# Where the adjacency's byte blocks are made in two fused graph-attention layers

## The chip, the cores and the metric

The kernel runs on one core of one Trainium2 chip. The time is the device time of one execution in microseconds (us); of several runs the median is given. A profile is one separate execution with the hardware profiler on. Engine names in the profile: PE is TensorE (PEld its weight loads), DVE is VectorE, ACT is ScalarE, POOL is GpSimd, SP is SyncE, which here only issues DMAs. A line such as L586 is a line of the kernel.

## The reference

A graph of 3327 nodes with 512 features passes two attention layers, then one binarized linear layer. Cut to what matters:

```python
for l in range(2):                                   # attention layers
    proj = x @ W[l]; Wh, Ws = split(proj, 2)         # 512 -> 2 x 512
    scores = Wh @ Ws.T                               # 3327 x 3327
    a = softmax(scores, axis=-1) * adj
    x = leaky_relu(a @ Wh + x, 0.01)
h = layernorm(x0 + x)
xw = max(sign(h), 0) @ sign(weight).T
out = layernorm(h + relu(adj @ xw))                  # adj once more
```

`adj` holds zeros and ones as 32-bit floats. All matmuls of the attentions are in 32-bit floats; the last product with `adj` is made from one-byte copies of `adj` and 16-bit values.

## The kernel before, in words

Scores are kept transposed: nodes j of the keys on the partitions, queries i along the free axis. The 26 tiles of 128 nodes form `NQ = 13` pairs. Every 256 x 256 block product, of scores and of values, is made with seven half-size products in place of eight (Strassen's scheme in Winograd's form), with sums of operands made beforehand. That is why each block has "sums" next to it.

A **full step** `(g, q)` is one 256 x 256 block: query pair g, key pair q; there are 169 of them in an attention, numbered i = 13 g + q. `values` (L820) makes its seven products into accumulators that live through a row g. Before that, in the steps ahead of it, the block goes through `shift` (L739: column maximum subtracted, DVE), `exponential` (L744, L745, ACT), `running` (L750: sum for the softmax, DVE), `masked` (L755: times `adj`, DVE) and `sums` (L793 to L796, POOL).

Scores run ahead of values by `LOOK = 30` half steps, because a row needs its maximum over all q before the first exponential. `ahead` lists these half steps: column block c (two rows g), key pair q, and s = 0 or 1. Half step s = 0 makes four of the seven products, s = 1 the other three (L586), into three banks `pZ`, `pX`, `pY`; ACT copies a bank out (L603, L638) before TensorE adds the next product to it, and DVE makes the final sums (L613, L628, L634) and the running maximum `top` (L654, L656). After the last q of a column block the maximum over the partitions is found by `column_max` (L687 to L707).

The loop over v runs from -34 to 168. In v the scores of half step u = v + 30 are made, and the values of step v if v is not negative. So **steps with scores alone** are v = -30 to -1; in them only scores and maxima are made, until the first rows' `shift` at v = -3. Within one v all work is sorted by a hand-written fraction (0.0 for `shift` of step v + 3, 0.12 for its exponential, 0.4 for `masked` of step v + 2, 0.6 to 0.62 for its byte block, and so on), and each engine gets its instructions in that order. The queues of SP and POOL are in order of issue too: in each v SP issues the load of `ws` (L801), then of `adj` for step v + 4 (L723; L115 and L117 where rows are cut), then `xs` and `gs` for the scores ahead (L577, L568).

The **byte blocks** are what the last layer needs of `adj`. Where an `adj` tile is on the chip anyway for `masked`, DVE makes four sums of its quarters as bytes (`halved_sums`, L775) and tests that all elements are zero or one (`exact`, L784), ACT casts three quarters (`halved`, L761, L762), and in the next v POOL writes the 112 KB block to memory (`keep_blocks`, L778). The byte tile `ab` has two buffers, the `adj` tile four. Each of the 169 blocks is made once: attention 0 makes those with q even (91), attention 1 those with q odd (78). Before, a block is made in its own step if g < 9; the blocks of rows 9 to 12 (28 and 24 of them) are spread over earlier steps of the other parity, which load a second `adj` tile for it.

The last rows of attention 1 and the last layer (L1134) follow; they are not touched.

## Time and profile before

| what | value |
|---|---|
| runs before (3) | median 2616.8 us, 2616.53 to 2617.85 |
| profiled execution | 2613.73 us, its span 2611.9 us |
| granted TensorE clock | 0.999 |
| first score product to first value product, attention 0 | 184.7 to 276.6 us |
| the same, attention 1 | 1400.5 to 1492.6 us |
| last value product of attention 1 | 2471 us |
| DMA moved | 639.15 MB, 245 GB/s on average |

The span runs from the first to the last instruction; the execution's time has 1.8 us around it. A busy TensorE is counted from the modelled ends of pipelined matmuls, so for lost time the count of matmuls in a window is the better measure. In the timeline a line gives start, duration, engine, line, operation, tiles and, in brackets, the idle time of the engine just before it and what ended it. Groups of byte-block work in the page:

```profile
L784 DVE SCALAR_TENSOR_TENSOR adj<-adj 128x512 f32<-128x512 f32 x169 | 139.8, 827 | 25.4 <-ACT ab L762 8.9 <-ACT u L603 0.5 <-DVE ab L775 0.5
L775 DVE TENSOR_TENSOR ab<-adj 128x128 fp8e4<-128x128 f32 x338 | 118.0, 349 | 29.2 <-DMA adj_d<-ab 28.6 <-POOL as L793 0.4
L775 DVE TENSOR_TENSOR ab<-adj,ab 128x128 fp8e4<-128x128 f32 x169 | 86.5, 512 | 0.0
L775 DVE TENSOR_TENSOR ab<-ab,adj 128x128 fp8e4<-128x128 fp8e4 x169 | 79.3, 469 | 5.8
```

The columns are line, engine, operation, tiles, shapes and count, then busy us and mean ns, then idle us before them by cause.

### The profile page before, as it was taken

The page shows a single profiled execution, that of the slowest core. Times are in us where ns is not written, and L with a number is a line of the kernel's source. Part 1 is how long each engine was busy: PE and PEld are TensorE (multiplying, and loading weights), DVE is VectorE, ACT ScalarE, POOL GpSimd, SP SyncE. Part 2 cuts the span into 40 slices and gives each one's busy share as a digit, 9 for nine tenths or more (in the row PEclk, how much of TensorE's full clock was granted, in tenths as well). Part 3 has the DMA queues.
Part 4 walks back from the last instruction along what each step waited for, and adds up shares of the span by engine and source line. Part 5 has one row for each costly group of instructions (what it writes and reads, how often), then busy time and mean ns, then how long its engine had stood idle before and what let it go on. Part 6 is the DMA issues. An engine that isn't in the chain of part 4 may idle for free. (4 is left out here: it accounts for less than half of the span.)

```text
span 2611.9 us, 40070 instructions
## 1 busy us (share of the span) xinstructions
PE 2578.8 (99%) x12511; PEld 2234.7 (86%) x12536; DVE 2109.5 (81%) x4422; ACT 799.8 (31%) x1978; POOL 1091.7 (42%) x2025
## 2 busy tenths in 40 slices
PE   9999999999999999999999999999999999999998
PEld 7888888888888888887888888888888888888787
DVE  6754888899888996768874689989899898777976
ACT  3323332333323332221332333333333333222143
POOL 3640343444434444456662044444444444454610
PEclk9999999999999999999999999999999999999999
DMA  6855777777777877698865678777787777678775
GB/s 216 293 193 180 241 241 265 241 268 251 261 240 236 276 239 237 223 265 252 300 242 179 224 225 283 249 250 258 239 281 247 246 263 237 231 260 262 262 252 182
DMA packets 309783, 639.15 MB, mean 245 GB/s; under 512 B 35048, under 2 KB 177986, under 8 KB 308027
## 3 DMA queue, kind: packets, MB, share of 16 engines
q1 hardware_dynamic: 273868, 530.29, 62.8%
q0 software_dynamic: 35664, 106.18, 11.0%
q8 instruction: 103, 1.69, 0.3%
q14 instruction: 118, 0.96, 0.1%
q10 hardware_dynamic: 30, 0.03, 0.0%
HBM read 529.69 MB, written 106.67 MB: 244 GB/s over the span
## 5 line engine op out<-in xcount | busy, mean ns | idle before, releaser
L586 PE MATMUL pZ<-gs,xs 128*128 128x256 f32 x2496 | 636.9, 379 | 3.0 <-ACT u L603 2.8
L793 POOL TENSOR_TENSOR as<-s 128x128 f32<-128x128 f32 x338 | 162.7, 481 | 1052.6 <-DVE s L755 873.2
L586 PEld LDWEIGHTS pZ<-gs,xs 128*128 128x128 f32 x2496 | 473.0, 190 | 71.3 <-ACT u L603 6.3
L820 PE MATMUL acc<-ws,s 128*128 128x256 f32 x1352 | 402.4, 379 | 0.1
L820 PE MATMUL acc<-wh,s 128*128 128x256 f32 x1352 | 355.7, 379 | 0.7 <-DVE s L755 0.4
L820 PE MATMUL acc<-ws,as 128*128 128x256 f32 x1352 | 348.0, 380 | 4.2 <-POOL as L795 4.1
L745 ACT ACTIVATE s<-s 128x512 f32<-128x512 f32 x338 | 213.2, 631 | 394.3 <-DVE s L739 393.3
L586 PE MATMUL pY<-gs,xs 128*128 128x256 f32 x1248 | 320.8, 379 | 6.0 <-ACT p L603 6.0
L820 PEld LDWEIGHTS acc<-ws,as 128*128 128x128 f32 x1352 | 256.1, 190 | 45.7 <-POOL as L795 8.6
L820 PEld LDWEIGHTS acc<-wh,s 128*128 128x128 f32 x1352 | 256.6, 190 | 36.7 <-DVE s L755 1.9
L820 PEld LDWEIGHTS acc<-ws,s 128*128 128x128 f32 x1352 | 255.7, 190 | 35.5 <-DVE h L855 1.3
L586 PEld LDWEIGHTS pY<-gs,xs 128*128 128x128 f32 x1248 | 236.6, 190 | 40.0 <-ACT p L603 7.9
L656 DVE TENSOR_TENSOR top<-top,s 128x512 f32<-128x512 f32 x286 | 199.9, 713 | 72.9 <-ACT s L643 52.6
L739 DVE TENSOR_TENSOR s<-s,off 128x512 f32<-128x512 f32 x338 | 246.8, 730 | 0.6
L755 DVE TENSOR_TENSOR s<-s,adj 128x512 f32<-128x512 f32 x338 | 239.5, 709 | 8.6 <-DMA adj<-in_adjT_dram 0.6
L750 DVE TENSOR_TENSOR total<-total,s 128x512 f32<-128x512 f32 x312 | 230.3, 738 | 0.0
L795 POOL TENSOR_TENSOR as<-s 128x128 f32<-128x128 f32 x338 | 202.1, 598 | 26.5
L603 ACT COPY u<-pZ 128x256 f32<-128x256 f32 x312 | 115.5, 370 | 308.0 <-PE pZ L586 304.9
L820 PE MATMUL acc<-wh,as 128*128 128x256 f32 x676 | 202.5, 381 | 0.0
L794 POOL TENSOR_TENSOR s<-s 128x128 f32<-128x128 f32 x338 | 182.9, 541 | 27.4
L796 POOL TENSOR_TENSOR as<-s,as 128x128 f32<-128x128 f32 x338 | 183.0, 541 | 26.5
L628 DVE TENSOR_TENSOR s<-p,u 128x256 f32<-128x256 f32 x156 | 66.5, 427 | 137.6 <-ACT u L603 136.9
(214 smaller groups left out, 3886.8 us busy)
## 6 DMA issues: line engine op xcount, KB each, us to landing
ws<-ws_d SPq DMA_DIRECT2D x338, 512.0 KB, 3.8
xs<-xs_d SPq DMA_DIRECT2D x182, 512.0 KB, 5.7
adj<-in_adjT_dram SPq DMA_DIRECT2D x324, 256.0 KB, 4.3
xs<-xs_d SPq DMA_DIRECT2D x156, 384.0 KB, 6.2
gs_d<-gsp POOLq DMA_DIRECT2D x88, 256.0 KB, 3.1
gs<-gs_d SPq DMA_DIRECT2D x12, 1792.0 KB, 10.9
adj_d<-ab POOLq DMA_DIRECT2D x169, 112.0 KB, 3.9
ahl<-adj_d SPq DMA_DIRECT2D x78, 224.0 KB, 5.0
```

The lines of the kernel that those rows point to most:

```text
L586: nc.tensor.matmul(ch[bank], xs[c, q, a][:, k], gs[c][:, b, k], start=(start and k == 0), stop=(k == 1), skip_group_check=True,)
L603: nc.scalar.copy(ch[name], ch[bank])
L656: nc.vector.tensor_tensor(top[i], top[i], t, ALU.max)
L739: nc.vector.tensor_tensor(s, s, off[g].to_broadcast([P, 2, HW]), ALU.subtract)
L745: nc.scalar.activation(sc[g, q], sc[g, q], AF.Exp)
L750: nc.vector.tensor_tensor(total[g], total[g], sc[g, q], ALU.add)
L755: nc.vector.tensor_tensor(s, s, adj[g, q], ALU.mult)
L793: nc.gpsimd.tensor_tensor(s3, a11, a21, ALU.subtract)
L794: nc.gpsimd.tensor_tensor(a21, a21, a22, ALU.add)
L795: nc.gpsimd.tensor_tensor(s2, a21, a11, ALU.subtract)
L796: nc.gpsimd.tensor_tensor(s4, a12, s2, ALU.subtract)
L820: nc.tensor.matmul(acc[g][i // 2][:, i % 2], a[i], b[i], start=(q == 0 and i % 2 == 0), stop=(q == NQ - 1), skip_group_check=True,)
```

## The change

The steps in which the blocks are made are chosen anew. Of each attention, 14 blocks are moved to the steps with scores alone: they get the keys -27, -25, ..., -1, so their `adj` is loaded at v = key - 4, they are made at v = key - 2 (-29 to -3), and written at v = key - 1. In attention 0 these are the blocks of rows 11 and 12. In attention 1 they are first the six blocks with q = 11 and g odd (in the steps with these keys a column maximum is found), and then the last eight of the others (row 12, and q = 9 and 7 of row 11). All other blocks are made in their own step, those of rows 9, 10 and, in attention 1, the first three of row 11 too. No full step makes a block of another step any more, so second loads of `adj` in full steps go: 28 and 24 extra loads become 14 and 14.

```diff
-        first = NQ * (NQ - 4)
         mine = [i for i, e in enumerate(steps) if e[1] % L == l]
-        room = [i for i, e in enumerate(steps[:first]) if e[1] % L != l][2:]
-        late = [i for i in mine if i >= first]
-        blocks = {i: steps[i] for i in mine if i < first}
-        blocks.update(
-            {room[n * len(room) // len(late)]: steps[i] for n, i in enumerate(late)}
-        )
+        alone = list(range(4 - LOOK, 1, 2))
+        moved = [i for i in mine if l and steps[i][1] == NQ - 2 and steps[i][0] % 2]
+        moved += [i for i in mine[::-1] if i not in moved][: len(alone) - len(moved)]
+        blocks = {i: steps[i] for i in mine if i not in moved}
+        blocks.update({i - 1: steps[j] for i, j in zip(alone, moved)})
...
             if 0 <= v + 4 < len(steps):
                 load_adj(*steps[v + 4])
-                if blocks.get(v + 4, steps[v + 4]) != steps[v + 4]:
-                    load_adj(*blocks[v + 4])
+            elif v + 4 in blocks:
+                load_adj(*blocks[v + 4])
...
-                of = blocks.get(v + 2)
-                if of:
-                    work += [
-                        (0.6, lambda: halved_sums(*of)), (0.62, lambda: exact(*of)),
-                        (0.61, lambda: halved(*of)),
-                    ]
-                    after.append((0.5, lambda of=of: keep_blocks(*of)))
+            if v + 2 in blocks:
+                of = blocks[v + 2]
+                work += [
+                    (0.6, lambda: halved_sums(*of)), (0.62, lambda: exact(*of)),
+                    (0.61, lambda: halved(*of)),
+                ]
+                after.append((0.5, lambda of=of: keep_blocks(*of)))
```

## The prediction

> **What bounds the kernel now.** I read the page's busy table, then the windows of 40 us over the whole span, then the waits of TensorE, the view of tile `ab`, and the timeline where TensorE had lost time.

> ```profile
> PE 2578.8 (99%) x12511; PEld 2234.7 (86%) x12536; DVE 2109.5 (81%) x4422; ACT 799.8 (31%) x1978; POOL 1091.7 (42%) x2025
> ```

> TensorE (PE) is busy for 99% of the span, so only its 33 us of gaps can be won. To place them I use the windows; their columns are stretch, length, then busy us (and count) of PE, PEld, DVE, ACT, POOL, then clock and DMA.

> ```profile
> 190.00:257.00 67.00, 67.00 (x312) 58.86 (x311) 28.11 (x55) 20.47 (x55) 0.00 (x0) 1.00 0.53 164
> 262.20:278.50 16.30, 15.39 (x70) 12.74 (x68) 15.54 (x46) 6.71 (x18) 1.94 (x4) 1.00 0.89 293
> 400.00:440.00 40.00, 38.53 (x179) 33.35 (x178) 36.12 (x92) 12.11 (x34) 15.14 (x31) 1.00 0.74 241
> 440.00:480.00 40.00, 38.42 (x176) 32.50 (x175) 37.44 (x78) 12.22 (x33) 17.09 (x33) 1.00 0.75 243
> 480.00:520.00 40.00, 40.00 (x187) 35.22 (x186) 33.56 (x74) 13.82 (x38) 17.95 (x36) 1.00 0.76 240
> 720.00:760.00 40.00, 38.57 (x179) 33.65 (x178) 35.60 (x90) 11.76 (x32) 15.16 (x30) 1.00 0.73 242
> 760.00:800.00 40.00, 37.20 (x171) 31.57 (x170) 36.14 (x74) 12.08 (x32) 16.72 (x33) 1.00 0.69 222
> 1478.20:1494.00 15.80, 15.74 (x72) 13.10 (x71) 15.14 (x43) 6.96 (x18) 2.42 (x6) 1.00 0.84 281
> 1800.00:1840.00 40.00, 39.40 (x184) 34.01 (x184) 37.46 (x86) 12.84 (x35) 16.89 (x35) 1.00 0.75 249
> 2120.00:2160.00 40.00, 39.38 (x184) 33.99 (x183) 37.32 (x90) 13.22 (x34) 14.62 (x31) 1.00 0.72 237
> ```

> An undisturbed 40 us holds 187.5 matmuls, 0.213 us each; a count below that is lost time. Four windows of attention 0 miss 8.5 + 11.5 + 8.5 + 16.5 = 45 matmuls, 9.6 us. 600 to 640 us misses 1.5 (0.3 us). In attention 1 two windows hold 184 where their neighbours hold 187 to 191: about 0.75 us each. In 190 to 257 us, steps with scores alone, nothing is missing, and DVE works 28 of 67 us.

> ```profile
>   DVE ab L775: 28.6, 20
>   ACT ab L761: 27.1, 14
> DMA to landing us min/median/max: 1.9/3.9/8.3
> ```
> ```profile
> 431.19 0.40 ACT L761 CAST ab<-adj 128x256 fp8e4<-128x256 f32 x1 [2.59 <-DMA adj_d<-ab]
> 431.70 0.36 ACT L603 COPY p<-pY 128x256 f32<-128x256 f32 x1
> 432.11 1.13 PE L586 MATMUL pY<-gs,xs 128*128 128x256 f32 x4 [1.47 <-ACT p L603]
> ```

> Here is the cause in attention 0. `ab` has two buffers; when blocks are made in three steps running (24, 25, 26 here) the third waits until the first has been written out. ScalarE (ACT) stands 2.59 us in front of its cast, the copy that frees TensorE's bank is queued behind it, and TensorE stops. DVE stands too, and is late with the `shift` that the next exponential needs; that gives the stops at 456 and 459 us. The same pair returns at 752 to 780 us.

> ```profile
> 277.57 0.63 ACT L745 ACTIVATE s<-s 128x512 f32<-128x512 f32 x1 [2.96 <-DVE s L739]
> 278.11 0.35 ACT L638 COPY s<-pZ 128x256 f32<-128x256 f32 x1
> 278.51 1.13 PE L586 MATMUL pX<-gs,xs 128*128 128x256 f32 x4 [0.86 <-ACT s L638]
> ```

> And here is the second place that matters, the change from score steps to full steps. From 262.2 us DVE works without a gap (15.54 of 16.30 us), ACT waits for DVE's `shift`, and a copy queued behind that exponential holds TensorE. At 271 and 278 us of attention 0, and three times between 1487 and 1499 us of attention 1, TensorE already stops for this chain, together about 2.7 us. It has no slack.

> [...] `xs` takes 3.0 to 4.1 us to land at 190 to 245 us and 7.5 us behind the 1.8 MB load of `gs` at 255 us.

> **The change part by part.** A block is four DVE sums, an exactness test (`exact`), two ACT casts (0.41 + 0.30 us), one POOL write. On DVE it takes 1.74 us where POOL is idle (431.19 to 432.93) and 2.57 us where POOL works (272.81 to 275.38).

> 1. Extra blocks in the steps of the other parity go: 28 in attention 0, 24 in attention 1, with as many second loads of `adj`. Blocks then stand in every second step; in attention 0 two adjoin only at row ends, never three, so the two `ab` buffers suffice and the DMA waits should vanish. In attention 1 the stops at 1834 and 2159 us come right after pairs (54, 55) and (106, 107), of which the first goes. Gain: 9.6 + 0.3 + 1.5 = 11.4 us; I leave 0.5 us for maxima and row ends, so -10.9. Bounds -9.5 and -11.7. The 24 `adj` loads saved net (6 MB of 639) cost no TensorE time now and gain nothing.

> 2. Fourteen blocks per attention go into the score steps, one every second step (6.05 us of TensorE). DVE there has 28.1 us of work in 67 us, 2.54 per 6.05; with 1.74 it is 4.3, hidden. In attention 1 `binary_weight` adds 1.1 us to four of these, 5.4 of 6.05: hidden. The casts fall in the gap of 1.35 us that ACT has between the copies of `u` and `s` (0.71 used): hidden; without that cover each would cost up to 0.4 us. POOL idles there.

> 3. The last two of them come at steps v = -5 and -3, after the saturated stretch has begun: one ahead of the column maximum and `shift` of block row 0, one between the first and second `shift`. DVE has nothing idle to give, so 2 x 1.74 = 3.5 us go onto the chain, plus about 0.2 us because `exact` also waits for the casts, which stand behind two exponentials. 3.7 us per attention, 7.4 in all. Bounds: 2.0 each (part absorbed) and 5.1 each (DVE at the POOL price 2.57). What is late next there is the same copy behind the same exponential.

> 4. The first load. The order of the built program shows SP now issuing the first moved `adj` ahead of the second step's `xs`, which before was loaded during the projection (about 62 us). Its buffer lies on the projection's weights, so SP waits for their last matmul. In attention 0 that block is the corner one (12, 12): its second DMA also waits for a POOL memset, in POOL's queue behind the last `ws_d` write:

> ```profile
> 186.36 0.54 POOL L417 DMA_DIRECT2D ws_d<-t  x1
> 188.37 24.49 SPq L577 DMA_DIRECT2D xs<-xs_d  x9
> ```

> 186.90, two memsets (0.10 + 0.31 us) and gaps give 187.5; two DMA issues (0.4 us each) bring `xs` to 188.4; 4.0 us to land, as the first of the nine took, and the weight load 0.2 give 192.6, where TensorE wants it at 190.76. Cost 1.8 us, bounds 1.0 and 3.0. In attention 1 there is no memset: SP is free at 1399.8, `xs` goes at 1400.3 and lands by 1405.3, wanted at 1406.4: nothing.

> 5. An `adj` load now follows `gs` of the second column block, ahead of `xs`, which landed at 262.36 for 263.37. 256 KB at the 270 GB/s of neighbouring windows is 0.95 us: 0.3 us, bounds 0 and 1. In attention 1 it landed at 1477.33 for 1479.2: nothing.

> 6. Blocks of rows 9 to 11 now stand in their own steps. DVE in 2280 to 2320 us works 34.3 of 40; three contended blocks add 7.7, a lag of 2 us that the next window (21.3 of 40) absorbs. The value products have room: row 0 is masked at 272.6 us and first used at 276.6. I take 0.8 us for both attentions, bounds 0 and 3. From step 149 on no block stands in either kernel, so the end of attention 1 and the final layer stay.

> Sum: -10.9 + 7.4 + 1.8 + 0.3 + 0.8 = -0.6 us. On the profiled execution, span 2611.9 and time 2613.73, this gives 2611.3 and 2613.1; the median of the runs is 3.1 us above that execution, so 2616.8 - 0.6 = 2616.2.

> **The rivals.** No change, by these offsetting parts, is the forecast. (A) The starts absorb the two late blocks, because TensorE's accumulator banks give more slack than the stops suggest: parts 3 and 4 fall to about 1 us. Then -10.9 + 2.1 = -8.8, 2608.0; half absorbed, -4.9 with 2612. For it speaks that DVE stays fully busy from 278 to 292 us (13.26 of 13.5) with TensorE hardly stopped; against it that TensorE does stop at both copies before. (B) The other side, slower: the starts cost more, because the late blocks meet POOL's sums and the casts enter ACT's chain as well: 2.57 + 0.71 us per block, 6.6 per attention, 13.2 in all. Then -10.9 + 13.2 + 2.9 = +5.2, 2622. It is slower than before from 4.0 us per attention on, and beyond 0.2% from about 6.6. Against it: POOL is idle until the first masked step, after both blocks. (C) The gain is half: stops at rows 2 and 6 come from maxima and residuals, not the `ab` wait. Then -5.5 + 10.3 = +4.8, 2621.6. Against it: similar row ends at 600 and 921 us lose 0.4 and 0.2 us, without such a wait.

> **How the numbers follow.** Forecast 0.62, (A) 0.22, (B) 0.09, (C) 0.07. A change of 0.2% is 5.2 us, about what a measurement tells from none. The forecast's own range, its bounds taken together, is 2612.5 to 2620. Faster by more: most of (A) and a little of the forecast, 0.22. Slower by more: half of (B) and (C) and the forecast's edge, 0.12. Within: 0.66. Range at 8 in 10: 2610 to 2620.5.

> **What would show it.** Right: no `ab` wait on `adj_d` among the full steps and 187 matmuls in 400 to 480 and 720 to 800 us (moved by a few us); an idle of about 1.8 us in front of the second `pZ` after the projection in attention 0, ended by `xs`; stops adding to some 5 us around v = -3 to 0 in each attention, behind ACT's exponential. Wrong: starts with the old 1.4 us, then (A); row ends still stopping, then (C).

## The result and the profile after

The changed kernel takes 2620.19 us (median of 22 runs, 2614.6 to 2622.36), the kernel before on the same chip 2615.53 us (22 runs). The ratio is 1.0018, its 95% interval 1.0012 to 1.0024: slower by 0.18%. The two profiled spans stand at 2617.7 and 2611.9 us, 5.8 us apart. The prediction's range, 2610 to 2620.5, holds the time, but by luck: it was counted from 2616.8 us, and this kernel before took 1.3 us less; 2616.8 + 4.7 would be 2621.5. Its reading, no change by offsetting parts, does not hold: -0.6 us was foreseen and +4.7 measured. That is a small change, but its interval leaves no change out.

The page of the changed kernel, busy us by engine (compare the first line of the prediction):

```profile
PE 2583.7 (99%) x12536; PEld 2239.9 (86%) x12536; DVE 2103.2 (80%) x4422; ACT 798.4 (31%) x1978; POOL 1117.7 (43%) x2023
```

TensorE's total says nothing of the cause. The next view does: windows of the changed kernel with the same columns as in the prediction, at the places where TensorE lost time before.

```profile
400.00:440.00 40.00, 40.00 (x187) 35.22 (x186) 33.87 (x81) 12.71 (x33) 17.11 (x33) 1.00 0.78 274
440.00:480.00 40.00, 40.00 (x188) 35.17 (x188) 35.94 (x72) 11.74 (x30) 17.84 (x33) 1.00 0.71 242
...
720.00:760.00 40.00, 40.00 (x187) 35.22 (x186) 35.44 (x87) 12.14 (x31) 15.84 (x32) 1.00 0.76 257
760.00:800.00 40.00, 40.00 (x188) 35.20 (x187) 35.02 (x69) 11.58 (x29) 18.66 (x35) 1.00 0.71 236
1800.00:1840.00 40.00, 40.00 (x191) 34.76 (x190) 33.11 (x78) 12.24 (x30) 14.80 (x28) 1.00 0.69 228
2120.00:2160.00 40.00, 40.00 (x190) 34.76 (x190) 32.73 (x78) 12.72 (x31) 15.90 (x30) 1.00 0.63 212
```

All hold full counts now: 187 or 188 where 171 to 179 stood, 190 and 191 where 184 stood. The gain is there, whole. So the loss must be larger than the gain, and elsewhere. To find it I cut both traces at the same four instructions of each attention (first score product, first product of steps 1 and 126, last value product) and compare the pieces. All are differences of start times in the two profiles, and the last columns are those of four experiments told below.

| piece | before, us | after | first load later | both edits | late rows too | three buffers |
|---|---|---|---|---|---|---|
| start of the program to first score product | 184.7 | +1.1 | +0.2 | 0.0 | +1.7 | +2.1 |
| attention 0, first score product to step 1 | 99.5 | +9.0 | +3.8 | +0.2 | 0.0 | 0.0 |
| attention 0, steps 1 to 126 | 766.8 | -10.7 | -10.7 | -10.7 | -10.3 | -8.8 |
| attention 0, steps 126 to the last | 191.1 | +2.6 | +3.3 | +5.0 | +0.3 | -0.2 |
| attention 1, first score product to step 1 | 99.6 | +5.3 | +3.5 | +0.5 | +0.1 | -0.2 |
| attention 1, steps 1 to 126 | 777.3 | -1.7 | -1.7 | -1.7 | -1.7 | 0.0 |
| attention 1, steps 126 to the last | 193.6 | +0.3 | +0.3 | +1.2 | +1.1 | 0.0 |

The pieces that are not in the table (between the attentions, and the last layer) differ by 0.2 us at most. The first row is no work of the change: it moves by up to 2.7 us between executions of all these kernels. Each column is one execution, and pieces that wait for transfers vary: in the kernel called "attention 1 alone" below, attention 0 is made as before, yet its steps 1 to 126 took 2.0 us less than here. So the changed kernel wins 12.4 us in the middle of the attentions and pays 14.3 at the two starts and 2.9 in the late rows. I go through these places now.

The first start in the timeline of the changed kernel (start, length, engine, line, operation, tiles, idle before and what ended it):

```profile
188.22 0.31 POOL L721 MEMSET adj<- 128x256 f32 x1
...
188.92 1.07 SPq L117 DMA_DIRECT2D adj<-in_adjT_dram  x1
...
190.04 0.93 SPq L577 DMA_DIRECT2D xs<-xs_d  x2
...
195.62 1.62 PE L586 MATMUL pZ<-gs,xs 128*128 128x256 f32 x3 [3.55 <-DMA xs<-xs_d]
```

This is the stop that part 4 of the prediction foresaw, with its whole chain: POOL's memset, SP's two `adj` DMAs behind it, then `xs`. But it lasts 3.55 us and not 1.8: `xs` landed at 195.48, 5.4 us after its issue, where 4.0 were assumed. Now `adj` loads issued at 188.6, 188.9 and 191.0 us and a second `xs` 0.4 us behind it are on the way at the same time (DMA share 0.85 in the first window below). And the stop has a tail. The next view is a set of windows of the changed kernel, cut at the 3.41 us steps in which the granted clock changes; the third figure from the end is that clock.

```profile
191.60:195.01 3.41, 0.46 (x3) 0.06 (x1) 1.75 (x7) 0.87 (x3) 0.65 (x2) 1.00 0.85 246
195.01:198.42 3.41, 2.80 (x7) 2.30 (x8) 0.00 (x0) 0.37 (x1) 0.00 (x0) 0.50 1.03 360
...
276.93:280.34 3.41, 1.71 (x7) 0.89 (x6) 3.09 (x11) 2.30 (x6) 0.00 (x0) 1.00 0.94 304
280.34:283.75 3.41, 3.41 (x9) 2.69 (x9) 3.31 (x8) 1.39 (x4) 0.84 (x2) 0.50 0.79 259
1481.83:1485.24 3.41, 1.32 (x7) 1.14 (x7) 2.40 (x8) 0.97 (x4) 0.54 (x1) 1.00 1.01 350
1485.24:1488.66 3.42, 3.42 (x10) 2.68 (x9) 3.26 (x10) 0.60 (x2) 0.00 (x0) 0.50 0.91 323
```

Three times a window in which TensorE stood for about half or more is followed by one at clock 0.50. There TensorE counts as busy (2.80, 3.41 and 3.42 us), yet makes 7, 9 and 10 matmuls; the window at 198.42 us, at full clock, makes 18. At half speed half of the busy time is lost: 1.4 + 1.7 + 1.7 = 4.8 us in all, which no idle time shows. In the profile of the kernel before no such window is recorded among its matmuls: the clock is 1.00 from 7.2 to 2604.7 us, and the last matmul ends at 2601.7 us.

The change from score steps to full steps, attention 0, in the timeline of the changed kernel:

```profile
277.03 0.69 DVE L739 TENSOR_TENSOR s<-s,off 128x512 f32<-128x512 f32 x1
...
278.31 0.28 DVE L775 TENSOR_TENSOR ab<-adj 128x128 fp8e4<-128x128 f32 x1
...
278.44 1.13 PE L586 MATMUL pX<-gs,xs 128*128 128x256 f32 x4 [1.14 <-DVE s L634]
...
280.13 1.91 PE L586 MATMUL pZ<-gs,xs 128*128 128x256 f32 x4 [0.56 <-ACT p L603]
...
281.46 0.68 DVE L739 TENSOR_TENSOR s<-s,off 128x512 f32<-128x512 f32 x1
```

The byte block at 278.31 stands between the first `shift` (277.03) and the second (281.46), as part 3 said, and TensorE stops for DVE's sums and for ACT's copies. The four matmuls at 280.13 take 1.91 us where those at 278.44 take 1.13: that is the half clock again.

Attention 1 stops elsewhere:

```profile
1470.23 0.43 SPq L568 DMA_DIRECT2D gs<-gs_d  x1
...
1470.77 0.38 SPq L723 DMA_DIRECT2D adj<-in_adjT_dram  x1
...
1473.32 2.91 SPq L577 DMA_DIRECT2D xs<-xs_d  x2
...
1484.00 1.10 PE L586 MATMUL pZ<-gs,xs 128*128 128x256 f32 x4 [2.08 <-DMA xs<-xs_d]
```

`xs` of the second column block came 10.55 us after its issue, behind a `gs` that took 11.66 us (6.47 and 8.28 before). Part 5 had put this at nothing for attention 1.

And the late rows, attention 0, step 130:

```profile
1064.98 0.29 DVE L775 TENSOR_TENSOR ab<-adj 128x128 fp8e4<-128x128 f32 x1
...
1067.34 1.03 DVE L697 COPY mx<-mxq 32x8 f32<-32x8 f32 x4
...
1070.82 0.42 DVE L847 TENSOR_TENSOR h<-acc,op 128x256 f32<-128x256 f32 x1 [0.35 <-ACT op L846]
...
1071.30 0.70 PE L820 MATMUL acc<-wh,s 128*128 128x256 f32 x2 [1.68 <-DVE h L847]
```

The blocks of keys 129 and 130 adjoin at the row's end, with the column maximum between and after them. DVE comes to the row's output (L847), which frees the accumulator, 1.68 us too late (0.35 us of it DVE itself waits for ACT).

### The profile page after: what moved, and what is told of

The parts are those of the page before. It is cut to its first block, busy times and chain, and to the rows that moved or that the text cites. A ratio compares the mean times of both kernels' runs of the same rounds, so it can differ in the third digit from the quotient of the medians.

```text
span 2617.7 us, 39989 instructions
## 1 busy us (share of the span) xinstructions
PE 2583.7 (99%) x12536; PEld 2239.9 (86%) x12536; DVE 2103.2 (80%) x4422; ACT 798.4 (31%) x1978; POOL 1117.7 (43%) x2023
## 5 line engine op out<-in xcount | busy, mean ns | idle before, releaser
L586 PE MATMUL pZ<-gs,xs 128*128 128x256 f32 x2496 | 639.6, 380 | 8.5 <-DMA xs<-xs_d 6.0
L586 PEld LDWEIGHTS pZ<-gs,xs 128*128 128x128 f32 x2496 | 475.1, 191 | 76.2 <-issue 3.9
L586 PE MATMUL pY<-gs,xs 128*128 128x256 f32 x1248 | 321.6, 380 | 0.0
L745 ACT ACTIVATE s<-s 128x512 f32<-128x512 f32 x338 | 213.4, 631 | 322.5 <-DVE s L739 321.0
L586 PEld LDWEIGHTS pY<-gs,xs 128*128 128x128 f32 x1248 | 237.9, 191 | 33.1 <-ACT p L603 0.3
L739 DVE TENSOR_TENSOR s<-s,off 128x512 f32<-128x512 f32 x338 | 251.2, 743 | 0.6
L603 ACT COPY u<-pZ 128x256 f32<-128x256 f32 x312 | 116.0, 372 | 383.2 <-PE pZ L586 383.2
L794 POOL TENSOR_TENSOR s<-s 128x128 f32<-128x128 f32 x338 | 198.9, 588 | 27.3
L796 POOL TENSOR_TENSOR as<-s,as 128x128 f32<-128x128 f32 x338 | 190.0, 562 | 26.5
## 6 DMA issues: line engine op xcount, KB each, us to landing
gs<-gs_d SPq DMA_DIRECT2D x12, 1792.0 KB, 10.7
```

The source lines that it names most:

```text
L586: nc.tensor.matmul(ch[bank], xs[c, q, a][:, k], gs[c][:, b, k], start=(start and k == 0), stop=(k == 1), skip_group_check=True,)
L739: nc.vector.tensor_tensor(s, s, off[g].to_broadcast([P, 2, HW]), ALU.subtract)
L745: nc.scalar.activation(sc[g, q], sc[g, q], AF.Exp)
L794: nc.gpsimd.tensor_tensor(a21, a21, a22, ALU.add)
L796: nc.gpsimd.tensor_tensor(s4, a12, s2, ALU.subtract)
```

## The experiments

The theory after the result ("starts"): the gain is the wait for `ab`, and the losses are the first load (with its half clock), the two late blocks' DVE time, and the late rows, each on its own. The rivals: one of these causes carries the others, or the gain comes from something else than the `ab` wait. A ratio is always to the kernel before on the same chip (medians 2616.1 us for the first four, 2614.86 for the last four), with its 95% interval.

**First load later.** The first moved block's `adj` is issued behind the second step's `xs`.

```diff
-            elif v + 4 in blocks:
+            elif v + 4 in blocks and v + 4 > min(blocks):
                 load_adj(*blocks[v + 4])
...
+            if v == -LOOK:
+                load_adj(*blocks[min(blocks)])
```

> The changed kernel with one edit: in each attention the adjacency load of the first moved block (key -27) is issued behind the load of the second step's xs in place of ahead of it. Theory 'starts': the stop at 195.6 us of attention 0 (3.55 us idle, then 3.4 us in which TensorE's clock is granted at one half, 5.1 us in all) and the 0.5 us at 1409 us go: 5 us less than the changed kernel, that is about 2615 us beside some 2615.5 of the kernel before; and no half clock near 195 us. If the half clock has another cause than the stop, only 3.5 us go (2616.7). Rival 'chain alone' (the prediction's size of this part, 1.8 us, was right and the rest is the DVE chain at the changes): at most 1.8 us less, 2618.4 or more.

Measured: 2613.51 us, ratio 0.9992 (0.9983 to 1.0). Against the changed kernel that is 1.0018 - 0.9992 = 0.26%, 6.8 us, where 5 us were expected. The windows of this kernel at the same place, columns as before:

```profile
191.60:195.01 3.41, 3.41 (x17) 3.02 (x16) 1.43 (x5) 1.24 (x4) 0.65 (x2) 1.00 0.91 299
195.01:198.42 3.41, 3.41 (x17) 2.99 (x16) 2.37 (x9) 1.62 (x6) 0.22 (x1) 1.00 0.71 233
```

Stop and half clock are both gone, and in this execution the other two half clocks too, so the rival (1.8 us at most) falls. What remains of the start, +3.8 and +3.5 us in the table, has no half clock in it and is almost what the prediction had for parts 3 and 5 (4.0 and 3.7).

**Two blocks back.** Twelve blocks in the score steps; those at v = -5 and -3 return to their own steps.

```diff
-        alone = list(range(4 - LOOK, 1, 2))
+        alone = list(range(4 - LOOK, -3, 2))
```

> The changed kernel with twelve blocks in the score steps of each attention in place of fourteen: the two made at v = -5 and -3 go back to their own full steps, and so no adjacency load stands behind gs of the second column block. Theory 'starts': the stops at 278 to 288 us (about 3.8 us with the half clock) and at 1484 to 1499 us (4.8 us) go: 8 us less than the changed kernel, less about 0.5 us for two more blocks in late rows, about 2612.5 us; the stop at 195 us stays. Rival 'first load alone' (the stops at the changes come from scores and maxima as before and only moved): under 2 us less, 2618 or more.

Measured: 2613.76 us, ratio 0.9991 (0.9983 to 1.0), 7.1 us less than the changed kernel, so the rival (under 2 us) falls. In its profile attention 1's start is back at +0.3 us; that of attention 0, still +6.7, keeps the first stop (3.69 us idle) and two windows at half clock after it. The late rows pay more than the 0.5 us expected: +3.9 and +1.1 where +2.6 and +0.3 stood. A block put back in a row whose steps are short is not free.

**Three byte buffers in the kernel before.** This asks whether the wait for `ab` is the cause of the gain.

```diff
-                [P, 7, P], F8, tag="adj_b", bufs=2, name=f"ab_{l}_{g}_{q}"
+                [P, 7, P], F8, tag="adj_b", bufs=3 if l == 0 else 2, name=f"ab_{l}_{g}_{q}"
```

> The kernel before with three byte-tile buffers (ab) in attention 0 in place of two, all blocks where they were. Theory of part 1 of the prediction (waits for the write-out of ab): the stops in 400 to 480 and 720 to 800 us go, 9 to 10 us less than the kernel before, about 2606 us. Rival 'half' (stops come from maxima and residuals at row ends): at most 5 us less. If the third buffer gives nothing, the cause of the gain in the changed kernel is DVE's load in those steps and not the wait.

Measured: 2606.48 us, ratio 0.9964 (0.995 to 0.9978): 9.6 us less than the kernel before. Windows of this kernel:

```profile
400.00:440.00 40.00, 40.00 (x187) 35.21 (x186) 35.97 (x91) 12.30 (x32) 16.53 (x33) 1.00 0.77 259
440.00:480.00 40.00, 39.92 (x186) 34.80 (x185) 38.89 (x79) 13.42 (x36) 18.04 (x35) 1.00 0.78 257
720.00:760.00 40.00, 40.00 (x188) 35.20 (x187) 35.94 (x90) 13.00 (x35) 16.75 (x33) 1.00 0.75 252
760.00:800.00 40.00, 39.85 (x185) 34.77 (x184) 38.93 (x80) 12.66 (x33) 18.80 (x38) 1.00 0.76 247
```

Every block is still made where it was, DVE is even busier (38.9 of 40 us), and TensorE is full. So most of the loss was the wait for the buffer, not DVE's load: rival (C) falls, and one more 112 KB buffer brings nearly what the change gained in attention 0 (10.7 us; in the table's piece it is 8.8, and no run isolates the other 1.9).

The wait alone does not make a stop, though. In the kernel before ACT also stood 5.04 us for `ab` at 399.5 us and 4.49 us at 719 us, longer than at 431, and TensorE did not stop: the windows from 360 to 400 and 680 to 720 us hold 188 matmuls each. At 431 us, where the copy that TensorE needed stood behind it, TensorE stopped for 1.47 us.

**Both edits**, first load later and twelve blocks.

```diff
-        alone = list(range(4 - LOOK, 1, 2))
+        alone = list(range(4 - LOOK, -3, 2))
...
-            elif v + 4 in blocks:
+            elif v + 4 in blocks and v + 4 > min(blocks):
...
+            if v == -LOOK:
+                load_adj(*blocks[min(blocks)])
```

> Both edits: twelve blocks in the score steps and the first of their loads behind xs. Theory 'starts': the sum of the two, 13 us less than the changed kernel, 2607 us, 8 to 9 us less than the kernel before. Left over are the late rows of attention 0 (2.8 us) against a gain of 12 us. Rival: if the two share a cause (both stops feed one delay that is absorbed once) the sum falls short by 4 us or more, 2611 or above.

Measured: 2608.09 us, ratio 0.9966 (0.9955 to 0.9977), 13.6 us less than the changed kernel. The two edits alone gave 6.8 and 7.1, so they add. Both starts are clean in the table (+0.2, +0.5); +5.0 us stays in the late rows of attention 0. This kernel and the one with two blocks back stop there for the same 2.01 us, and show what a half clock is. First the kernel with two blocks back:

```profile
1067.03:1070.44 3.41, 1.99 (x9) 1.78 (x10) 3.02 (x8) 1.17 (x3) 1.13 (x3) 1.00 0.85 273
1070.44:1073.85 3.41, 3.41 (x18) 2.73 (x17) 3.41 (x7) 0.13 (x1) 1.97 (x4) 1.00 0.37 145
```

then the one with both edits:

```profile
1058.77:1062.18 3.41, 1.40 (x7) 0.92 (x6) 2.96 (x9) 1.16 (x3) 0.00 (x0) 1.00 0.65 196
1062.18:1065.59 3.41, 3.41 (x9) 2.71 (x9) 3.38 (x9) 0.00 (x0) 2.95 (x6) 0.50 0.76 289
```

In the first the stop is split by the window's edge and only 1.43 us of it lie in the window shown; the clock stays. In the second all 2.01 us lie in one window, and the next makes 9 matmuls in place of 18. By the matmuls the same stop costs 2 us in one execution and near 4 in the other; the whole pieces, other small stops included, differ by 1.1 us (+3.9 and +5.0).

**Late rows.** Both edits, and three blocks of rows 10 and 11 of attention 0 made earlier.

```diff
+        if l == 0:
+            for j, i in ((130, 105), (143, 96), (145, 100)):
+                blocks[i] = blocks.pop(j)
...
                 load_adj(*steps[v + 4])
+                if blocks.get(v + 4, steps[v + 4]) != steps[v + 4]:
+                    load_adj(*blocks[v + 4])
```

It also has the third buffer of attention 0, as above.

> The kernel with both edits (twelve blocks, first load behind xs), and in attention 0 three blocks of rows 10 and 11 (keys 130, 143, 145) made in earlier steps of the other parity (keys 105, 96, 100), with a third byte-tile buffer so that three in a row do not wait. Theory 'DVE in late rows' (blocks that adjoin in steps of 4.7 us make DVE late with the row's output, and TensorE stops 2.0 us at 1061 us of attention 0 and 1.1 us after it): the stop of 2.2 us at the start of step 130 falls to 0.5 or less, and with it any half clock behind it: 2 to 4 us less than with both edits, 2604 to 2606 us. Rival 'the row's end itself' (column maximum and residual, whatever the blocks): under 0.5 us.

Measured: 2604.77 us, ratio 0.9963 (0.9949 to 0.9976). Each median against its own kernel before, this is 10.1 - 8.0 = 2.1 us better than both edits; the two intervals overlap, so the time alone doesn't show it. The profile does: the stop at the end of row 9 is gone, and the piece after step 126 falls from +5.0 to +0.3 us. The same 16 us with both edits, then in this kernel:

```profile
1055.00:1071.00 16.00, 13.99 (x58) 11.68 (x57) 15.11 (x38) 3.84 (x11) 8.16 (x15) 0.89 0.58 189
1055.00:1071.00 16.00, 16.00 (x77) 14.05 (x76) 15.22 (x37) 3.86 (x10) 7.18 (x14) 1.00 0.73 249
```

The third buffer is not what does it: with both edits no wait for the write-out of `ab` stands at this row's end; DVE has work without a gap from 1050 us on until 0.35 us before the row's output at 1061.2 us.

**Three buffers, no pairs.** The kernel with three buffers, and in attention 1 the extra blocks beside the column maximum moved by one step.

```diff
+        if l == 1:
+            blocks[56], blocks[108] = blocks.pop(54), blocks.pop(106)
```

> The kernel before with three byte-tile buffers in attention 0, and in attention 1 the two extra blocks of keys 54 and 106 made at keys 56 and 108. Theory (a block of the other parity next to the column maximum makes DVE late): the two stops of 0.73 us at 1827 and 2152 us go, 1.5 us less than with three buffers alone, about 2605 us. Rival: the stops follow the blocks to the next step, 0 us.

Measured: 2604.57 us, ratio 0.9963 (0.995 to 0.9977), by time not to be told from three buffers alone. First the windows of three buffers alone:

```profile
1800.00:1840.00 40.00, 39.43 (x187) 34.32 (x186) 37.30 (x79) 12.48 (x33) 15.81 (x31) 1.00 0.79 264
2120.00:2160.00 40.00, 39.43 (x184) 34.39 (x183) 37.34 (x85) 12.14 (x32) 16.81 (x36) 1.00 0.76 250
```

and those of this kernel:

```profile
1800.00:1840.00 40.00, 40.00 (x191) 35.00 (x190) 36.18 (x76) 12.89 (x35) 16.08 (x30) 1.00 0.80 260
2120.00:2160.00 40.00, 40.00 (x191) 35.13 (x190) 36.77 (x82) 12.12 (x33) 15.63 (x32) 1.00 0.81 266
```

Both stops are gone: steps 1 to 126 of attention 1 take 1.6 us less, as expected, and no stop took their place. The wait for `ab` was not their cause: here DVE stands 1.60 us and ACT 2.85 us for it at 1831 us, more than before those stops, and TensorE does not stop. This kernel and late rows are the fastest here, some 10 us below the kernel before and 14 to 15 below the changed one.

**Attention 1 alone.** Attention 0 as before (the old choice of steps kept there), attention 1 as changed.

```diff
+        if l == 0:
...
+            blocks = {i: steps[i] for i in mine if i < 117}
+            blocks.update(
+                {room[n * len(room) // len(late)]: steps[i] for n, i in enumerate(late)}
+            )
...
+                if blocks.get(v + 4, steps[v + 4]) != steps[v + 4]:
+                    load_adj(*blocks[v + 4])
```

> Attention 0 as in the kernel before, attention 1 as in the changed kernel. Theory 'starts': attention 1 gains 1.7 us at two row ends and gives back 3.3 us (the DVE chain of the two late blocks) and up to 2 us more where gs lands late: 1.6 to 4 us slower than the kernel before. Rival 'prediction' (3.7 + 0.4 - 1.5, no other stop): 2.6 us slower; rival 'absorbed': faster by 1 us. The stop at 1409 us (0.5 us, xs of the second step) and the one at 1499 us are to be seen again.

Measured: 2618.09 us, ratio 1.0012 (1.0005 to 1.0018), 3.2 us slower. Attention 1 loses by the change on its own. The profile has +3.9 us at the start, nearly all in stops behind DVE and ACT between 1488 and 1503 us and none at the second column block's `xs`, -1.7 at the row ends and +0.3 after. These pieces add to +2.5 us: the time can't tell "starts" from the prediction's own 2.6, which held in this execution, where `gs` of attention 1 landed in good time (8.21 us here, 11.66 in the changed kernel's profile).

**Late blocks untested.** First load later, and the test (L784) left out for the two late blocks (POOL writes a zero in place of its count).

```diff
...
-                    (0.6, lambda: halved_sums(*of)), (0.62, lambda: exact(*of)),
+                    (0.6, lambda: halved_sums(*of)),
+                    (0.62, lambda: (exact if v + 2 not in (-3, -1) else untested)(*of)),
```

> The changed kernel with the first load behind xs, and the test for zeros and ones left out for the two blocks made at v = -5 and -3 of each attention: 0.9 us of DVE less for each. That part of the computation is missing. Theory 'DVE chain' (every microsecond of DVE put there is a microsecond of TensorE): 1.8 us less in each attention, 3.6 us less than with the first load behind xs alone, 2609.9 us; the stops at 264 to 283 us fall from 4.6 to about 2.8 us. Rival 'ACT or transfers' (the casts in ACT's order, or the late xs): under 1 us in all.

Measured: 2608.56 us, ratio 0.9978 (0.9969 to 0.9988). Against first load later that is 0.9992 - 0.9978 = 0.14%, 3.7 us (3.6 expected). By pieces the starts fall from +3.8 and +3.5 to +2.2 and +1.7 us, so 1.6 and 1.8 for 1.8 us of DVE work taken out. (In attention 1 of this execution 0.76 us of what is left is a new wait for `xs`.) Windows of 26 us over the change to full steps in attention 0, first load later:

```profile
264.00:290.00 26.00, 22.37 (x99) 18.46 (x100) 24.67 (x67) 9.25 (x26) 8.35 (x15) 1.00 0.75 242
```

the same without the two tests:

```profile
264.00:290.00 26.00, 23.55 (x107) 19.45 (x106) 23.87 (x66) 10.54 (x30) 7.82 (x15) 1.00 0.81 272
```

and with no late blocks (both edits):

```profile
264.00:290.00 26.00, 25.37 (x116) 22.05 (x117) 25.06 (x64) 9.88 (x26) 8.37 (x15) 1.00 0.72 233
```

99, 107, 116 matmuls: with less block work on DVE there, TensorE gets more done. The rival (casts or transfers, under 1 us) falls.

## Why the prediction was right in its parts and wrong in its sum

- **Part 1 right, a little small.** Predicted -10.9 us, measured -10.7 and -1.7. Even 11.4, the sum before 0.5 us was kept back for row ends, falls 1.0 short. Three buffers alone show that the main cause in attention 0 was the `ab` wait (9.6 us by the medians against the 9.9 predicted).
- **Part 2 right for the engines.** In 200 to 250 us TensorE makes 232 matmuls with the blocks (both edits) and 233 without. What it didn't count is traffic: the DMA share there goes from 0.49 to 0.72.
- **Part 3 right.** 3.7 us per attention were predicted. With the first load out of the way, so that nothing else delays the start, +3.8 (with part 5) and +3.5 us are measured, and taking out half of the DVE work takes out about half of it. Rival (A), that the starts absorb, is refuted, and so is (B), 6.6 us per attention, as a cost of the chain. The sum ended near (B)'s 2622, for another reason.
- **Part 4 is the step that failed.** Its order was right and its price was not: "Cost 1.8 us, bounds 1.0 and 3.0", and 3.55 us of idle time and 1.4 us of half clock measured, 5.0 in all. Counted from the first score product, the memset came when it should; the second `adj` DMA took SP 1.07 us for 0.4, so that `xs` left 4.2 us after that product and not 3.7; and the landing took 5.4 us for 4.0. That figure came from a time when no `adj` load was on the way, and the change itself put some there: over the ten profiles the first `xs` issued after the first score product of attention 0 lands in 4.0 to 4.1 us where no blocks are moved (four) and in 4.6 to 5.5 us where they are (six). 1.8 + 0.5 + 1.4 is 3.7, about the stop. For the clock after it the sum had no term. In attention 1, where the part had nothing, `xs` took 6.6 us for the 5.0 allowed, and TensorE stood 0.3 us.
- **The missing term, half clock.** In the two profiled executions it is the miss: the pieces of the table add to -12.4 + 14.3 + 2.9 = +4.8 us, and the three half clocks are 4.8. Without them the sum would be zero, near the forecast, because the gain and the late rows, both larger than predicted, happen to cancel. But this is one execution of the changed kernel. Its mean granted clock is 0.997: the three windows cost 5.1 us of clock, the stretch after the last matmul 3.0. Of the 22 runs, 17 show 0.998 and one 0.999. At 0.998 at most 6.5 us are lost, and the end alone took 2.3 us or more in all ten profiles, so these runs had at most two such windows. And the four runs at 0.997 (2618.7 to 2619.74 us) are below the median, not above it. How the median's +4.7 us divides between half clock and stops stays open.
- **Part 5 too small, and not for the cause it names.** In attention 0 no wait for this `xs` stands, where 0.3 us was put. In attention 1 TensorE waits at the second column block for 2.08 us in the changed kernel, but for 1.50 us with both edits too, where no `adj` load stands behind `gs`, and not at all in attention 1 alone, where it does. Over these profiles `gs` took 7.8 to 10.1 us to land where no blocks are moved (seven cases) and 8.2 to 11.7 where they are (thirteen). The traffic in the score steps (DMA share in 200 to 250 us: 0.49 without the blocks, 0.72 with them) may be the cause; no run isolates it, so it stays open.
- **Part 6 too small.** 0.8 us predicted, 2.6 and 0.3 measured, 2.9 in all. The estimate took DVE's average over 40 us; the stop comes from one place where two blocks adjoin with a column maximum, in steps of 4.7 us, and the late-rows kernel shows it by taking one of the two away.
- **A slip that changes nothing.** With parts 3 and 4 half absorbed, rival (A)'s own terms give -4.7 and not -4.9 us.

## What to carry to other kernels

Before work is moved off a crowded stretch, ask what the crowd is waiting for: here it was a buffer, and a third one gave 9.6 us where moving the work gave a loss of 4.7. Work moved ahead of a phase brings its loads with it, and here the new transfers went with slower landings of the old ones (4.6 to 5.5 us for 4.0 to 4.1). Issuing the first of them behind what TensorE needed next gave 6.8 us. A stop of TensorE is not priced by its length alone: the same 2.01 us cost 2 us in one execution and near 4 in another, where 3.41 us at half clock followed, so the matmuls after a stop have to be counted too. And the terms of one profile should be held against the clocks and times of all runs before they are taken for the median.

## What the runs showed of the hardware

```profile
1068.81:1072.22 3.41, 1.73 (x8) 1.22 (x7) 2.99 (x8) 1.17 (x3) 0.23 (x1) 1.00 0.57 197
1072.22:1075.64 3.42, 3.42 (x17) 2.71 (x17) 3.42 (x7) 0.00 (x0) 2.88 (x6) 1.00 0.80 305
```

One window that was itself at half clock, with 1.61 us idle (two blocks back), was followed by another at half clock. No run was made to set the idle time by hand, so the border is what these stops happened to show.
